# One image's group norm issued as three steps instead of one, its square on another engine, and a new order of issue

## The chip, the cores and the metric

The kernel runs on one core of a Trainium2 chip. A core has five engines that work side by side, each through its own instruction queue in order: TensorE (PE, with its weight loads PEld), VectorE (DVE), ScalarE (ACT), GpSimd (POOL), and SyncE (SP), which here only issues DMA transfers. Engines wait for each other through semaphores. The metric is the time of the whole launch on the device in microseconds (us); lower is better.

## The reference

The input is 16 images of 64 x 64 pixels with 128 channels, float32. Two layers follow each other, each a residual around a group norm over 32 groups of 4 channels:

```
g = v.reshape(B_, H_, W_, G, C_ // G)
m = mean(g, axis=(1, 2, 4));  s = var(g, axis=(1, 2, 4))
_gn(v) = (g - m) / sqrt(s + 1e-5)

x = x + L0(_gn(x))        # layer 0: a two-dimensional recurrent cell over rows and columns
x = x + L1(_gn(x))        # layer 1: a selective state space model (Mamba), forward and backward
```

Layer 1 flattens an image to 4096 tokens. Both directions share the weights. Per direction: a projection to 256 inner channels and a depthwise convolution of 4 taps with silu give `xc`; from `xc` come a small `dt` (softplus), and 16 values each of B and C per token. For each of 256 channels and 16 states a recurrence runs over the tokens,

```
h = exp(dt * A) * h + dt * B * xc
y = sum over states of h * C   (+ xc * D)
```

and `y` times a silu gate is projected back to 128 channels. The two directions are added.

## The kernel before

**Layer 0** takes the first 1,500 us or so: a wavefront over the diagonals of the images, eight images at a time. The square of its norm is the same code as in layer 1. Its cell has a product on GpSimd (L892) beside one on VectorE (L893).

**Layer 1** is the rest. An image is 16 passes: eight chunks of 512 tokens forward (the first half), then the same eight backward (the second half). A chunk is held as two halves of 128 channels on the partitions. For each pass and half, the exponentials `da` (L1248, "decay") are made by ScalarE; the recurrence of one state over 512 tokens is one VectorE scan (L1305, 32 a pass). Four of the 16 states (those below NX) get `dt*x*B` from GpSimd (L1256, `group`), the other twelve from TensorE by diagonal matrices (L1285, `hps`). Twelve products with C are made by GpSimd (L1328, `hc`), two states each; with `dt*x` (L1229) and four products with B that is 18 GpSimd instructions a pass. TensorE sums the states by transposing (L1365). The last value of each scan goes by a small DMA from SP (L1317, "keep") to `carry`, for the next pass. A pair of scans shares a buffer `hst`, of which there are three.

**The next image's norm.** While image b is scanned, image b+1 is read chunk by chunk (read_load, read_turn, read_take, read_stats): loaded, transposed by TensorE, copied to `xT` by ScalarE, and its statistics taken by VectorE (L1061). When all eight are there, `normal` (L1063) combines them and calls `group_norm` (L730): mean over the four channels of a group by a matmul, deviation on VectorE, its square on ScalarE, variance by two matmuls, square root on ScalarE (L743), reciprocal and shift on VectorE. Then `normalise` (L1073) applies scale and shift to the eight chunks on ScalarE. There are 15 such norms in the scan layer, one for each image but the first, whose norm ends layer 0. ScalarE's functions lie in tables; the square root's and the exponential's are not loaded together.

**The order of the work** is written by a planner that runs before the kernel is built. `order_of_issue` lists every operation of layer 1 with its engine, a cost from the table COST, what it comes after, and which ring buffers it takes and releases; `simulate` plays them and picks on each engine, whenever it is free, the ready operation with the lowest key. The key is NS times the pass number plus a number from the table URGENCY, one for each operation of a pass and for each half. An operation may have a `table`; then TABLE (1.28) is added where ScalarE's table changes. The result is one list in which all engines' instructions are issued; on the chip each engine works through its part in order, and a waiting instruction holds up all behind it. Three PSUM banks ("bank") are shared by transposes, projections and the decays of four states.

To the planner `normal` is one operation of VectorE of 3.0 us without a table, although it also issues TensorE's and ScalarE's parts at that place.

Of the kernel before, what the change touches and what calls it, by code (L numbers as in the profile page):

```python
# [9 lines left out]
AF = mybir.ActivationFunctionType  # L10
ALU = mybir.AluOpType
# [33 lines left out]
def units_of(order):  # L45

    count = {}
    for x in order:
# [4 lines left out]
        else:  # L53
# [18 lines left out]
    "read_take": 0.56, "read_stats": 0.69, "normal": 3.0, "normalise": 0.75, "spread": 0.6, "rows": 1.0,  # L72
# [18 lines left out]
        {(0, 0): 68.37, (0, 1): 99.65, (0, 2): 79.28, (0, 3): 203.77, (1, 0): -114.87, (1, 1): -118.67,  # L91
         (1, 2): -126.73, (1, 3): -118.24},
        {(0, 0): 155.27, (0, 1): 154.99, (0, 2): 240.19, (0, 3): 214.32, (1, 0): -240.9, (1, 1): -234.27,
         (1, 2): -200.93, (1, 3): 192.92},
    ),
    "xproj": (
        {(): -10.97},
        {(): 44.2},
    ),
    "xproj_take": (  # L100
        {(): -8.7},
        {(): 67.11},
    ),
    "rows": (
        {(): -153.13},
        {(): -118.25},
    ),
    "bturn": (
        {(): 62.15},
        {(): 213.27},  # L110
    ),
    "bturn_take": (
        {(): 172.77},
        {(): 178.75},
    ),
    "dtproj": (
        {(0,): -204.87, (1,): -204.87},
        {(0,): -241.05, (1,): -56.88},
    ),
    "times": (  # L120
        {(0,): -244.38, (1,): 220.24},
        {(0,): -131.05, (1,): -34.21},
    ),
    "turn": (
        {(0,): 249.35, (1,): 249.17},
        {(0,): -12.52, (1,): 136.36},
    ),
    "turn_take": (
        {(0,): 225.5, (1,): 225.64},
        {(0,): 168.68, (1,): 229.12},  # L130
    ),
    "scaled": (
        {(0,): 241.23, (1,): 249.64},
        {(0,): -126.09, (1,): 207.32},
    ),
    "skip": (
        {(0,): 219.33, (1,): 133.55},
        {(0,): -198.84, (1,): 234.94},
    ),
    "spread": (  # L140
        {("b", 0): 100.66, ("d", 0): 113.55, ("c", 0): -191.38, ("c", 1): -175.48, ("d", 1): -182.63,
         ("c", 2): -137.51, ("c", 3): 194.71, ("b", 1): 239.03, ("d", 2): -6.3, ("c", 4): 205.44, ("c",
         5): 205.67, ("k", 0): 249.62},
        {("b", 0): -196.06, ("d", 0): -21.03, ("c", 0): 95.8, ("c", 1): 217.74, ("d", 1): -173.2, ("c",
         2): -224.87, ("c", 3): -109.91, ("b", 1): 32.51, ("d", 2): 68.11, ("c", 4): 105.18, ("c", 5):
         250, ("k", 0): 106.72},
    ),
    "drive": (
        {(0, 0): -29.51, (1, 0): -31.7, (0, 1): 248.1, (1, 1): 247.61},
        {(0, 0): -30.69, (1, 0): -14.83, (0, 1): 76.36, (1, 1): 227.82},  # L150
    ),
    "decay": (
        {(0, 0): 118.09, (4, 0): 46.1, (5, 0): 43.31, (6, 0): 225.59, (7, 0): 236.9, (1, 0): 231.93, (8,
         0): 212.64, (9, 0): 250, (10, 0): 220.73, (11, 0): 230.04, (2, 0): 219.52, (12, 0): 250, (13,
         0): 243.2, (14, 0): 242.1, (15, 0): 236.57, (3, 0): 92.3, (4, 1): 244.91, (5, 1): 245.08, (6,
         1): 230.56, (7, 1): 235.88, (0, 1): 94.2, (8, 1): 250, (9, 1): 250, (10, 1): 249.86, (11, 1):
         249.41, (1, 1): 240.77, (12, 1): 94.69, (13, 1): 246.36, (14, 1): 95.9, (15, 1): 250, (2, 1):
         250, (3, 1): 250},
        {(0, 0): 143.92, (4, 0): 173.94, (5, 0): 235.37, (6, 0): 166.71, (7, 0): 249.54, (1, 0): 211.4,
         (8, 0): 218.32, (9, 0): 181.78, (10, 0): 227.93, (11, 0): 238.08, (2, 0): -85.83, (12, 0):  # L160
         229.6, (13, 0): 219.86, (14, 0): 178.16, (15, 0): 196.66, (3, 0): 76, (4, 1): 209.87, (5, 1):
         236.73, (6, 1): 35.09, (7, 1): 155.05, (0, 1): 65.39, (8, 1): 246.13, (9, 1): 249.07, (10, 1):
         45.55, (11, 1): 213.12, (1, 1): 199.94, (12, 1): 249.37, (13, 1): 240.07, (14, 1): 201.6, (15,
         1): 223.57, (2, 1): 139.92, (3, 1): 139.64},
    ),
    "scan": (
        {(0, 0): -143.97, (4, 0): -144.41, (5, 0): -203.2, (6, 0): -177.82, (7, 0): -185.62, (1, 0):
         -181.51, (8, 0): -237.82, (9, 0): -224.86, (10, 0): -250, (11, 0): -238.04, (2, 0): -238.15,
         (12, 0): -228.87, (13, 0): -229.22, (14, 0): -249.94, (15, 0): -248.9, (3, 0): 6.49, (4, 1):
         138.6, (5, 1): 138.89, (6, 1): 21.72, (7, 1): 20.73, (0, 1): 168.47, (8, 1): 100.86, (9, 1):  # L170
         72.61, (10, 1): 93.86, (11, 1): 202.9, (1, 1): -199.43, (12, 1): -147.92, (13, 1): -148.63, (14,
         1): -181.73, (15, 1): -152.26, (2, 1): -134.86, (3, 1): -124.94},
        {(0, 0): -214.33, (4, 0): -219.13, (5, 0): -218.95, (6, 0): -219.13, (7, 0): -140, (1, 0):
         -246.02, (8, 0): 208.31, (9, 0): 184.92, (10, 0): 207.89, (11, 0): 205.81, (2, 0): 205.48, (12,
         0): 229.6, (13, 0): 227.38, (14, 0): 227.3, (15, 0): 227.84, (3, 0): 210.13, (4, 1): 203.18, (5,
         1): 190.13, (6, 1): 196.98, (7, 1): 248.22, (0, 1): 44.78, (8, 1): 44.3, (9, 1): 53.53, (10, 1):
         53.41, (11, 1): 53.08, (1, 1): 229.32, (12, 1): 226.23, (13, 1): -82.64, (14, 1): -82.71, (15,
         1): -47.78, (2, 1): -33.84, (3, 1): -110.83},
    ),
    "scatter": (  # L180
        {("d", 0): -100.64, ("d", 1): 95.72, ("d", 2): -159.12, ("k", 0): 102.97},
        {("d", 0): -25.83, ("d", 1): 239.18, ("d", 2): -120.64, ("k", 0): 187.06},
    ),
    "drive_rows": (
        {(0, 0): -75.98, (1, 0): 210.15, (2, 0): 159.44, (0, 1): -216.43, (1, 1): 95.52, (2, 1): 115.92},
        {(0, 0): 175.76, (1, 0): 119, (2, 0): -243.29, (0, 1): -177.54, (1, 1): 61.32, (2, 1): 235.16},
    ),
    "keep": (
        {(0, 0): 232.07, (1, 0): 115.13, (2, 0): 84.57, (3, 0): -18.36, (4, 0): 78.14, (5, 0): -150.63,
         (0, 1): 129.78, (1, 1): 176.01, (2, 1): -242.19, (3, 1): -198.85, (4, 1): 171.84, (5, 1): 202.73},  # L190
        {(0, 0): -91.43, (1, 0): 202.39, (2, 0): 250, (3, 0): -79.2, (4, 0): -18.6, (5, 0): 222.86, (0,
         1): -21.3, (1, 1): 184.5, (2, 1): -137.27, (3, 1): -121.94, (4, 1): -128.43, (5, 1): 158.96},
    ),
    "out_of": (
        {(0, 0): 220.21, (1, 0): 220.3, (2, 0): 247.6, (3, 0): 247.25, (4, 0): -116.32, (5, 0): -229.45,
         (0, 1): -18.17, (1, 1): -15.17, (2, 1): -16.71, (3, 1): -16.75, (4, 1): -16.1, (5, 1): -15.52},
        {(0, 0): -8.58, (1, 0): -16.15, (2, 0): 69.62, (3, 0): 56.3, (4, 0): 227.32, (5, 0): 43.54, (0,
         1): -112.29, (1, 1): -195.82, (2, 1): -184.49, (3, 1): -212.68, (4, 1): -240.92, (5, 1): 67.09},
    ),
    "sums": (  # L200
        {(0, 0): -96.07, (1, 0): 249.75, (2, 0): 243.85, (3, 0): 61.49, (4, 0): 172.81, (5, 0): -65.92,
         (0, 1): 147.15, (1, 1): 40.49, (2, 1): 16.98, (3, 1): -10.84, (4, 1): -198.17, (5, 1): -49.98},
        {(0, 0): -224.96, (1, 0): -243, (2, 0): -210.02, (3, 0): -250, (4, 0): -246.13, (5, 0): -82.21,
         (0, 1): 103.84, (1, 1): 150.23, (2, 1): 247.44, (3, 1): 191.91, (4, 1): 200.85, (5, 1): 136.54},
    ),
    "keep_group": (
        {(0, 0): -22.23, (0, 1): -187.05},
        {(0, 0): -239.66, (0, 1): -160.74},
    ),
    "turned": (  # L210
        {(0, 0, 0): -144.95, (0, 0, 1): 152.62, (0, 0, 2): -158.13, (0, 0, 3): -41.49, (0, 1, 0):
         -190.27, (0, 1, 1): -150.04, (0, 1, 2): -93.55, (0, 1, 3): -142.02},
        {(0, 0, 0): -247.79, (0, 0, 1): 84.82, (0, 0, 2): 79.27, (0, 0, 3): -247.36, (0, 1, 0): 202.59,
         (0, 1, 1): 200.35, (0, 1, 2): 199.96, (0, 1, 3): 200.1},
    ),
    "turned_take": (
        {(0, 0, 0): 25.04, (0, 0, 1): 26.28, (0, 0, 2): 24.39, (0, 0, 3): 95.62, (0, 1, 0): 136.51, (0,
         1, 1): 250, (0, 1, 2): 248.1, (0, 1, 3): 250},
        {(0, 0, 0): 88.31, (0, 0, 1): 231.98, (0, 0, 2): 231.27, (0, 0, 3): 200.95, (0, 1, 0): 171.58,
         (0, 1, 1): 167.45, (0, 1, 2): 165.18, (0, 1, 3): 210.27},  # L220
    ),
    "weigh": (
        {(0, 0): -37.82, (0, 1): 224.4},
        {(0, 0): 108.42, (0, 1): 136.29},
    ),
    "finish": (
        {(0,): 151.14, (1,): 250},
        {(0,): 141.5, (1,): -236.48},
    ),
    "spill": (  # L230
        {(): -28.08},
        {},
    ),
    "read_load": (
        {(): -189.73},
        {},
    ),
    "read_turn": (
        {(): -56.24},
        {},  # L240
    ),
    "read_take": (
        {(): 23.65},
        {},
    ),
    "read_stats": (
        {(): 53.18},
# [53 lines left out]
def order_of_issue(images):  # L301
# [27 lines left out]
    get = done.get  # L329
# [1171 lines left out]
```

## Time and profile before

| what | value |
|---|---|
| median of 3 runs | 12480.04 us (12465.78 to 12492.38) |
| the profiled execution's own time | 12473.08 us |
| its span | 12471.1 us |
| mean granted TensorE clock | 0.985 |
| busy: PE, DVE, ACT, POOL | 11816.2, 11102.2, 10217.3, 10573.6 us |
| one image in the scan layer | about 682 us |

The span is the time from the first instruction to the last. Busy time is that of an engine's own instructions; an idle time is put down to what ended it ("<-"). In a timeline a row is the start in us, the duration, the engine, the line, the operation with its tiles, and how many instructions were merged; in brackets stands the idle time before it and its releaser. In a table of stretches each engine has its busy time and, in brackets, its number of instructions.

### The profile page before, as it was taken

Reading aid. Unit: us, or ns where it says so; the run is one execution under the profiler, and the core shown is the slowest. Engines: PE = TensorE matmul, PEld = TensorE weight load, DVE = VectorE, ACT = ScalarE, POOL = GpSimd, SP = SyncE. Lnnn points to the kernel's source line nnn. Section 1 sums busy time; section 2 is a strip of 40 time slices with the busy share of each in tenths; the row PEclk is TensorE's granted clock in tenths of the full one; section 3 lists DMA queues with packets and bytes.
Section 4 is the critical chain, followed back from the end, with each engine's and each line's share of the span. In section 5 each row is a group of like instructions: output and inputs, shape, how many; then the busy total and the mean of one; then the engine's idle time right before and its main releaser. Section 6 shows DMA issues by size and latency. Waiting matters only on the chain. (4 is left out here: it accounts for less than half of the span.)

```text
span 12471.1 us, 314271 instructions
## 1 busy us (share of the span) xinstructions
PE 11816.2 (95%) x123700; PEld 9141.1 (73%) x123700; DVE 11102.2 (89%) x11407; ACT 10217.3 (82%) x16448; POOL 10573.6 (85%) x4868
## 2 busy tenths in 40 slices
PE   9999989999999989899999999998999999999989
PEld 8656867777777767677777777776777777777777
DVE  7767589899999999999999999999999999999989
ACT  3444588888888888888888888888888888898888
POOL 0111199999999999999999999999999999999999
PEclk9999899999999999999999999999999999999999
DMA  4222255555555555555555555555555555555555
GB/s 156 56 56 56 56 152 167 159 166 161 163 167 157 169 158 164 158 170 158 165 163 163 160 164 167 155 167 158 167 158 169 160 162 164 163 165 162 163 154 149
DMA packets 2333045, 1885.43 MB, mean 151 GB/s; under 512 B 1549985, under 2 KB 1895601, under 8 KB 2331569
## 3 DMA queue, kind: packets, MB, share of 16 engines
q1 hardware_dynamic: 2253616, 1830.09, 51.0%
q10 hardware_dynamic: 77952, 35.24, 1.2%
q8 instruction: 977, 16.01, 0.5%
q14 instruction: 500, 4.09, 0.1%
HBM read 1698.25 MB, written 164.30 MB: 149 GB/s over the span
## 5 line engine op out<-in xcount | busy, mean ns | idle before, releaser
L1328 POOL TENSOR_TENSOR hc<-hst,cr 128x1024 f32<-128x1024 f32 x3072 | 7391.7, 2432 | 421.5 <-DVE hst L1305 303.8
L1305 DVE TENSOR_TENSOR_SCAN hst<-da,carry,hps 128x512 f32<-128x512 f32 x5376 | 6449.9, 1261 | 489.5 <-issue 188.4
L1248 ACT ACTIVATE da<-dt,A_log_sb 128x512 f32<-128x512 f32 x8192 | 5409.2, 711 | 805.3 <-DVE hst L1305 717.8
L1365 PE MATMUL py<-ident,hc 128*128 128x128 f32 x24576 | 3207.3, 277 | 31.8 <-POOL hc L1328 30.9
L1365 PEld LDWEIGHTS py<-ident,hc 128*128 128x128 f32 x24576 | 2812.4, 143 | 516.2 <-issue 346.6
L1256 POOL TENSOR_TENSOR group<-dtx,br 128x1024 f32<-128x1024 f32 x1024 | 2464.3, 2408 | 19.8 <-DMA br<-rows 10.4
L1305 DVE TENSOR_TENSOR_SCAN group<-da,carry,group 128x512 f32<-128x512 f32 x1792 | 2234.4, 1266 | 161.0 <-ACT da L1248 159.8
L1285 PEld LDWEIGHTS hps<-d,dtxt 32*128 32x128 f32 x49152 | 1545.4, 189 | 936.2 <-issue 583.1
L1285 PE MATMUL hps<-d,dtxt 32*128 32x128 f32 x49152 | 1835.7, 286 | 395.6 <-issue 237.0
L1127 PE MATMUL pp<-xT,wk 128*128 128x512 f32 x4096 | 1946.3, 595 | 0.9 <-DVE xl L913 0.5
L1345 ACT COPY ht<-ptg 128x512 f32<-128x512 f32 x2048 | 1125.7, 588 | 322.5 <-PE ptg L1337 290.3
L892 POOL TENSOR_TENSOR a_f<-a_f,c 128x16 f32<-128x16 f32 (+35 forms) x254 | 188.4, 742 | 1320.4 <-ACT a_f L884 1258.0
L1337 PE MATMUL ptg<-ident,group 128*128 128x128 f32 x8192 | 1193.6, 281 | 59.8 <-ACT ht L1345 33.8
L1337 PEld LDWEIGHTS ptg<-ident,group 128*128 128x128 f32 x8192 | 935.6, 143 | 283.4 <-issue 98.8
L1127 PEld LDWEIGHTS pp<-xT,wk 128*128 128x128 f32 x4096 | 696.9, 191 | 487.5 <-issue 481.0
L1305 DVE TENSOR_TENSOR_SCAN hst<-da,hps 128x512 f32<-128x512 f32 x768 | 875.3, 1200 | 77.1 <-issue 41.0
L1229 POOL TENSOR_TENSOR dtx<-dt,xc 128x512 f32<-128x512 f32 x512 | 651.7, 1288 | 124.8 <-ACT dt L1223 95.9
L1248 ACT ACT_TABLE_LOAD x527 | 676.1, 1283 | 9.3
L1352 PE MATMUL py<-ht,k 128*32 128x128 f32 x16384 | 568.0, 277 | 22.2 <-ACT ht L1345 22.2
L884 ACT ACTIVATE a_f<-pg_f,b_sb 128x16 f32<-128x16 f32 (+35 forms) x508 | 220.0, 473 | 419.1 <-DMA x<-xl 208.7
L1213 PE MATMUL pv<-dbl,dt_wT 128*128 128x256 f32 x2048 | 531.4, 392 | 0.0
L1352 PEld LDWEIGHTS py<-ht,k 128*32 128x32 f32 x16384 | 414.0, 110 | 112.0 <-issue 43.2
(113 smaller groups left out, 12180.2 us busy)
## 6 DMA issues: line engine op xcount, KB each, us to landing
cr<-rows SPq DMA_DIRECT2D x1536, 512.0 KB
d<-d SPq DMA_DIRECT2D x768, 448.0 KB
br<-rows SPq DMA_DIRECT2D x512, 512.0 KB
k<-k SPq DMA_DIRECT2D x256, 256.0 KB
yf<-y SPq DMA_DIRECT2D x128, 512.0 KB
yl<-yf SPq DMA_DIRECT2D x128, 512.0 KB
carry<-hst SPq DMA_DIRECT2D x3072, 1.0 KB
xs<-in_x_dram SPq DMA_DIRECT2D x64, 512.0 KB
```

Source lines behind the costliest of these rows:

```text
L1127: nc.tensor.matmul(self.ps["conv", h], lhsT=wk[:, k, h * P : (h + 1) * P], rhs=xT[self.b % 2][:, t0 : t0 + T], start=(k == 0), stop=(k == ...
L1213: nc.tensor.matmul(pv[:, q * TQ : (q + 1) * TQ], lhsT=dt_wT[:, q, h * P : (h + 1) * P], rhs=self.dbl, start=True, stop=True,)
L1229: nc.gpsimd.tensor_mul(self.dtx[h], self.dt[h], self.xc[h])
L1248: nc.scalar.activation(t, self.dt[h], AF.Exp, scale=amat[:, h, s : s + 1])
L1256: nc.gpsimd.tensor_mul(both[:, m : m + 2, :], bc(self.dtx[h], 1, 2), self.brow[q])
L1285: nc.tensor.matmul(part[:, j, :, :], lhsT=self.dtxt[h][rows, j, :], rhs=dg[rows, j + r, :, :], start=True, stop=True, skip_group_check=True,)
L1305: nc.vector.tensor_tensor_scan(t[:, self.rev], self.da.pop((s, h))[:, self.rev], dbx[:, self.rev], 0.0 if self.first else carry[:, self.d, ...
L1328: nc.gpsimd.tensor_mul(self.hc[g, h], self.hst[g, h].rearrange("p t m -> p m t"), self.crow[g])
L1337: nc.tensor.transpose(pt[:, k, :], self.group[g, h][:, t0 : t0 + TB, :].rearrange("p t s -> p (t s)"), ident,)
L1345: nc.scalar.copy(t, self.ps.pop(("turned", g, h, j)))
L1352: nc.tensor.matmul(self.py[h][q * TB : (q + 1) * TB, j * P : (j + 1) * P], lhsT=cd[:, GX * j + q, :], rhs=self.ht[g, h, j][:, q, :], start ...
L1365: nc.tensor.matmul(self.py[h][:, cols], **{"start": False, "stop": False, **how}, skip_group_check=True)
```

## The change

The function `group_norm` is cut into `variance` (up to the variance in PSUM), `root` (the square root) and `affine` (reciprocal and shift). In the scan layer the three are separate operations for the planner: `normal` of 1.9 on VectorE, `root` of 0.26 on ScalarE with the table "sqrt", `affine` of 0.32 on VectorE. The PSUM bank is held until `affine` has read it. Layer 0 and the first image still call all three in a row. The square is a product on VectorE instead of an activation on ScalarE. All numbers of URGENCY are new, so the order of the whole scan layer is planned anew. The product dt*x stays on GpSimd.

```diff
-    "read_take": 0.56, "read_stats": 0.69, "normal": 3.0, "normalise": 0.75, "spread": 0.6, "rows": 1.0,
+    "read_take": 0.56, "read_stats": 0.69, "normal": 1.9, "root": 0.26, "affine": 0.32, "normalise": 0.75, "spread": 0.6, "rows": 1.0,
...
 URGENCY = {
...
     "scatter": (
-        {("d", 0): -100.64, ("d", 1): 95.72, ("d", 2): -159.12, ("k", 0): 102.97},
-        {("d", 0): -25.83, ("d", 1): 239.18, ("d", 2): -120.64, ("k", 0): 187.06},
+        {("d", 0): -168.23, ("d", 1): 82.53, ("d", 2): -166.69, ("k", 0): 97.09},
+        {("d", 0): -57.95, ("d", 1): 171.82, ("d", 2): -166.2, ("k", 0): 182.23},
     ),
...
     "normal": (
         {},
-        {(): 52.85},
+        {(): -21.8},
+    ),
+    "root": (
+        {},
+        {(): -78.05},
+    ),
+    "affine": (
+        {},
+        {(): -45.32},
     ),
     "normalise": (
         {},
-        {(): 87.21},
+        {(): 117.4},
     ),
...
                     put("normal", (), "DVE", who=b + 1, key=("normal", b + 1),
                         after=[get((f, b + 1, k)) for k in range(NCH) for f in ("read_take", "read_stats")], takes=[m],
-                        uses=[m])
+                        uses=[])
+                    tiles[m][1] += 1
+                    put("root", (), "ACT", who=b + 1, key=("root", b + 1), after=[get(("normal", b + 1))])
+                    ops[-1]["table"] = "sqrt"
+                    put("affine", (), "DVE", who=b + 1, key=("affine", b + 1), after=[get(("root", b + 1))])
+                    ops[-1]["uses"].append(m)
                 put("normalise", (n - NCH,), "ACT", who=b + 1,
-                    after=[get(("normal", b + 1))])
+                    after=[get(("affine", b + 1))])
...
-    def group_norm(pool, mv, n, tag, bank):
-
+    def variance(pool, mv, n, tag, bank):
...
-        nc.scalar.activation(sq, dev, AF.Square)
+        nc.vector.tensor_mul(sq, dev, dev)
         nc.tensor.matmul(pv, lhsT=gavg, rhs=sq, start=True, stop=False)
         nc.tensor.matmul(pv, lhsT=gavg, rhs=mv[:, :, 1], start=False, stop=True)
+        return pm
+
+    def root(pool, pm, n, tag):
+
         std = pool.tile([P, n], F32, name=f"std_{tag}", tag="gn_std")
-        nc.scalar.activation(std, pv, AF.Sqrt, bias=eps)
+        nc.scalar.activation(std, pm[:, 1, :], AF.Sqrt, bias=eps)
+        return std
+
+    def affine(pool, pm, std, n, tag):
+
         scale = pool.tile([P, n], F32, name=f"scale_{tag}", tag="gn_scale")
         nc.vector.reciprocal(scale, std)
         shift = pool.tile([P, n], F32, name=f"shift_{tag}", tag="gn_shift")
-        nc.vector.scalar_tensor_tensor(shift, mean, -1.0, scale, ALU.mult, ALU.mult)
+        nc.vector.scalar_tensor_tensor(shift, pm[:, 0, :], -1.0, scale, ALU.mult, ALU.mult)
         return scale, shift
...
         def normal(b, place=None):
             mv = gp.tile([P, 1, 2], F32, name=f"mv_{b}", tag="mv")
             nc.vector.bn_aggr(mv[:, 0, :], norm[b].rearrange("p n s -> p (n s)"))
-            norm[b] = group_norm(
-                gp, mv, 1, f"l1_{b}", lambda name, shape: bank(place, name, shape)
-            )
+            norm[b] = variance_of(gp, mv, 1, f"l1_{b}", lambda name, shape: bank(place, name, shape))
+
+        def root(b):
+            norm[b] = norm[b], root_of(gp, norm[b], 1, f"l1_{b}")
+
+        def affine(b):
+            norm[b] = affine_of(gp, *norm[b], 1, f"l1_{b}")
```

## The prediction

> **What bounds the kernel now.** I read the groups of instructions first. In the scan layer GpSimd does the two products of each state pair, and their rows are the largest:
>
> ```profile
> L1328 POOL TENSOR_TENSOR hc<-hst,cr 128x1024 f32<-128x1024 f32 x3072 | 7391.7, 2432 | 421.5 <-DVE hst L1305 303.8
> ...
> L1256 POOL TENSOR_TENSOR group<-dtx,br 128x1024 f32<-128x1024 f32 x1024 | 2464.3, 2408 | 19.8 <-DMA br<-rows 10.4
> ```
>
> With the 651.7 us of dt*x (L1229) that is 10,508 us. GpSimd's first product of this layer starts at 1,539 us and the last ends at 12,461, so it is busy 96% of 10,922 us. A pass has 18 such instructions, about 41 us. What is left to win is its idle time. So I cut image 10 (8,368 to 9,051 us) into stages; the columns are length, then busy time (count) of PE, PEld, DVE, ACT and POOL, then TensorE clock and DMA:
>
> ```profile
> 8452.10:8502.00 49.90, 42.60 (x489) 34.29 (x489) 42.92 (x40) 46.67 (x73) 42.22 (x20) 0.93 0.53 151
> ...
> 8543.70:8711.00 167.30, 147.97 (x1728) 114.49 (x1726) 150.31 (x126) 141.09 (x221) 158.96 (x72) 0.98 0.56 154
> 8711.00:9051.50 340.50, 337.86 (x3760) 264.75 (x3757) 318.56 (x281) 296.59 (x461) 326.69 (x145) 0.99 0.58 168
> ```
>
> The last line is the eight passes of the second half: PE is busy 337.9 of 340.5 us, POOL 326.7. They run at PE's pace and have nothing to give. The middle line is four passes of the first half, close to POOL's pace. The first line is the pass in which the next image's norm lies: 49.9 us instead of about 41.5, and no engine is full. What a first half costs without the next image's reads and norm is seen in the last image, which has none (first line below) against the image before it:
>
> ```profile
> 11777.60:12115.30 337.70, 307.53 (x3531) 240.39 (x3530) 305.54 (x259) 290.44 (x457) 324.20 (x146) 0.97 0.56 154
> 11095.50:11439.50 344.00, 310.28 (x3570) 241.91 (x3569) 311.41 (x271) 303.37 (x477) 324.00 (x145) 0.98 0.56 157
> ```
>
> So reads, norm and normalising together cost 6.3 us an image, 15 times: 95 us is the most that a better border can bring with the rest as it is. Then the timeline of one border (image 14), by engine, VectorE first, ScalarE next, GpSimd last:
>
> ```profile
> 11180.48 0.35 DVE L1065 BATCH_NORM_AGGREGATE mv<-st 128x2 f32<-128x48 f32 x1
> 11182.63 0.16 DVE L737 TENSOR_TENSOR dev_l<-mv,pm_l 128x1 f32<-128x1 f32 x1 [1.80 <-PE pm_l L735]
> 11184.63 0.16 DVE L745 RECIPROCAL scale_l<-std_l 128x1 f32<-128x1 f32 x1 [1.84 <-ACT std_l L743]
> 11184.83 0.16 DVE L747 SCALAR_TENSOR_TENSOR shift_l<-pm_l,scale_l 128x1 f32<-128x1 f32 x1
> 11184.91 4.79 DVE L1305 TENSOR_TENSOR_SCAN hst<-da,carry,hps 128x512 f32<-128x512 f32 x4
> 11189.99 2.46 DVE L1305 TENSOR_TENSOR_SCAN group<-da,carry,group 128x512 f32<-128x512 f32 x2 [0.29 <-ACT da L1248]
> 11193.15 1.28 DVE L1305 TENSOR_TENSOR_SCAN group<-da,carry,group 128x512 f32<-128x512 f32 x1 [0.70 <-ACT da L1248]
> ```
> ```profile
> 11182.82 0.20 ACT L739 ACTIVATE sq_l<-dev_l 128x1 f32<-128x1 f32 x1 [1.79 <-DVE dev_l L737]
> 11183.04 1.28 ACT L743 ACT_TABLE_LOAD   x1
> 11184.34 0.26 ACT L743 ACTIVATE std_l<-pm_l,eps 128x1 f32<-128x1 f32 x1
> ```
> ```profile
> 11187.53 4.79 POOL L1328 TENSOR_TENSOR hc<-hst,cr 128x1024 f32<-128x1024 f32 x2 [3.35 <-DVE hst L1305]
> 11197.01 2.43 POOL L1328 TENSOR_TENSOR hc<-hst,cr 128x1024 f32<-128x1024 f32 x1 [4.69 <-DVE hst L1305]
> ```
>
> VectorE is held from 11,180.48 to 11,184.99, 4.51 us without a scan: 1.80 idle for TensorE's mean, 1.84 for ScalarE's root. ScalarE idles 1.79 for the deviation. GpSimd then starves twice, 3.35 and 4.69 us; the other borders show the same pair.
>
> **The change part by part**, for one border, then times 15.
>
> *The hold of VectorE.* It loses the 1.84 us wait for the root, with the two last operations, which come later as a step of their own (0.36 us), and gains the square (0.16 us, the row of the deviation, same shape). The wait of 1.80 for the mean stays: the matmul stands in TensorE's queue behind its 32 block products. Counted so, VectorE gains 1.84 - 0.16 = 1.68 us.
>
> [...] The square multiplies the deviation by itself, both in SBUF; the deviation before it and the scans have an input in PSUM. [...]
>
> ```profile
> 993.48 1.19 POOL L892 TENSOR_TENSOR a_f<-a_f,c 128x472 f32<-128x472 f32 x1 [6.88 <-ACT a_f L884]
> ...
> 993.98 1.19 DVE L893 TENSOR_TENSOR a_f<-a_f,c 128x472 f32<-128x472 f32 x1 [1.84 <-ACT a_f L884]
> 995.27 0.65 DVE L895 TENSOR_TENSOR a_f<-a_f,a_f 128x472 f32<-128x472 f32 x1
> ```
>
> The same shape costs VectorE 1.19 us beside GpSimd and 0.65 alone; it ends 0.5 us after GpSimd's. In the scan layer GpSimd's instructions last 2.43 us, one after another. At the end of the 15 deviations the running one had between 0.12 and 1.94 us to go, mean 1.29. [...] I take 1.45: the hold becomes 4.51 - 1.84 - 0.36 + 1.45 = 3.76, the two last operations are paid later, and VectorE gains 0.4 us, not 1.7. Affine may also wait: nothing if the root is done when its turn comes, up to 1.84 if it is planned too early; I take 0.2 for it. Left: 0.2 us.
>
> *ScalarE.* The square and the idle time ahead of it go: 0.20 + 1.79 = 1.99 us. The root comes as a step of its own. The planner thinks that the variance is there 1.9 + 0.2 us after the norm starts; by the rows above it is there after 2.3 (deviation) + 1.45 + 0.4 (two matmuls) = 4.2. If the root is issued as soon as the plan allows, ScalarE waits the difference of 2.1 less the table load of 1.28 ahead of it, 0.8. Behind it stand the normalising steps and the decays that VectorE's scans wait for. So it gains 1.2 (bounds: 0 to 2.0). What that is worth: after the border VectorE waits 0.29 + 0.70 = 1.0 us for decays, so at most 1.0.
>
> *Table loads.* There is one for the root and one back to the exponential, 1.28 us each, as now; the plan before charged neither, the plan after charges both. A root set beside a table switch of the silu or softplus steps saves one. [...] I take the trace and a chance of one half: 0.65.
>
> *Hidden edits.* None of the three steps issues a DMA. The norms of the first layer (two) and the first image's also square on VectorE; a few tenths once each, in a span of 12,471: nothing. The PSUM bank is held from the mean to affine, some 6 us instead of 3; two of the three banks stay for the others. Bounds 0 to 1 us an image, taken as 0: if the cover of TensorE's backlog is gone, it is GpSimd that waits.
>
> *The order.* All urgencies are new, so every queue may differ: SP's keeps, scatters and spreads among them. I can't derive the order by reading. The second half is held by PE's sum of work whatever the order, the first by GpSimd's. I cost it at nothing, from -3 us an image (half of the 6.3) to +6 (second rival).
>
> **Sum.** 0.2 + 1.0 + 0.65 = 1.85 us x 15 = 28 us. The profiled execution took 12,473.1 us, its span 12,471.1 with 2 us around it; 12,473 - 28 = 12,445. The median of the runs shown is 7 us above that execution, so about 12,450.
>
> **The rivals.**
> *The border closes.* If the plan with its true costs also places decays and normalising so that GpSimd keeps its backlog, both gaps go: the bound is 95 us, 12,385. For it: ScalarE is busy 46.7 of 49.9 us there. Against: VectorE still does eight statistics of 0.67 us and the norm, about 9 us more than a plain pass, with 3 us of slack a pass.
> *The new order makes SP late, and it ends slower.* VectorE's rows of waits hold 157 us in all for `carry<-hst`: the small transfers that keep a last state, issued by SP in order, behind scatters that take 2.8 us for four. A scan pair can't write its buffer (three of them) until that transfer has read it. In the last image three first-half passes take 44.2 to 44.7 us for this, against 41.5. Two more passes of this kind in each of 16 images cost 2 x 2.7 x 16 = 86, less the 28: 12,540. It decides from about one such pass an image (2.7 against 1.85 us).
> [...]
>
> **How the numbers follow.** Within 0.2% (25 us) a measurement of this kernel can hardly tell a change from none. Forecast 0.35, its own range 12,420 to 12,470, of which four fifths lie below 12,455; border closed 0.14; stall only moved 0.16; SP late 0.35. Faster: 0.28 + 0.14 = 0.42. Same: 0.07 + 0.16 = 0.23. Slower: 0.35. The range goes from just below the border's bound, 12,380, to 12,580, which leaves the worst of the SP case, three and more passes, outside.
>
> **What would show it.** The hold from the aggregate to the square's end near 3.8 us, with the square's row well above 0.16 us (mean 1.0 to 1.5). No idle of 1.8 us ahead of the reciprocal. The root's row with a wait below 1 us; 527 + 256 + 255 + 18 table loads or some 8 fewer. The pass with the norm at 47 to 48 us, the second half at 340. I am wrong if VectorE's waits for `carry<-hst` rise well above 157 us, if second-half passes leave 42.5 us, or if the square stays at 0.16 and the pass falls below 45.

## The result, and the profile after

The changed kernel takes 12,517.9 us (median of six, 12,505.8 to 12,527.7), the kernel before on the same chip 12,471.0 (12,461.0 to 12,492.4): a ratio of **1.0035 (95% interval 1.0025 to 1.0045)**. It is slower by some 45 us, where 28 us faster were forecast. The time lies inside the range given, on the wrong side.

The profiled execution of the changed kernel, its fastest, has a span of 12,504.1 us against 12,471.1. The difference of 33 us is the sum of three: the scan layer begins at 1,551.1 instead of 1,539.0 us (+12, see the last section), the sixteen first halves take 5,479.1 instead of 5,497.5 (-18), the second halves 5,463.5 instead of 5,424.3 up to the last GpSimd product (+39; the tail behind it is 10.4 us in both). A pass is 18 GpSimd products, from the start of its first to that of the next pass's first. Images and passes are counted from 0: pass 2 is the third, pass 8 the first of the second half. Mean lengths over images 1 to 14, in us:

| profile | pass 1 | pass 2 (norm) | passes 3 to 7 together | pass 8 |
|---|---|---|---|---|
| before | 43.5 | 49.8 | 210.0 | 41.9 |
| changed | 45.9 | 50.0 | 206.4 | 43.8 |

So the pass with the norm, in which the whole gain was to appear, has not become shorter. The stretches of image 10 in the changed kernel, with the same columns as for the kernel before (length, busy time and count of PE, PEld, DVE, ACT, POOL, then TensorE clock, DMA share and GB/s): pass 2, and the second half.

```profile
8468.80:8518.60 49.80, 42.48 (x486) 32.57 (x487) 44.33 (x40) 44.59 (x70) 41.73 (x20) 0.97 0.54 147
...
8726.90:9068.60 341.70, 336.85 (x3737) 262.70 (x3737) 316.70 (x279) 294.75 (x458) 325.24 (x146) 1.00 0.57 167
```

ScalarE lost 2.1 us of busy time in that pass (46.67 before), but the pass still takes 49.8 us. The timeline of the border in image 14 shows what took its place. VectorE:

```profile
11209.89 0.34 DVE L1092 BATCH_NORM_AGGREGATE mv<-st 128x2 f32<-128x48 f32 x1
11210.76 0.15 DVE L751 TENSOR_TENSOR dev_l<-mv,pm_l 128x1 f32<-128x1 f32 x1 [0.54 <-PE pm_l L749]
11210.95 1.83 DVE L753 TENSOR_TENSOR sq_l<-dev_l 128x1 f32<-128x1 f32 x1
...
11216.24 0.13 DVE L767 RECIPROCAL scale_l<-std_l 128x1 f32<-128x1 f32 x1
...
11219.86 4.80 DVE L1336 TENSOR_TENSOR_SCAN hst<-da,carry,hps 128x512 f32<-128x512 f32 x4 [3.29 <-PE hps L1316]
```

The waits for the mean (1.80 us) and the root (1.84) have shrunk to 0.54 and to none. The square takes 1.83 us, and it ends at 11,212.78. GpSimd's timeline tells why: the second of its two products there ends at 11,212.77.

```profile
11208.04 4.73 POOL L1287 TENSOR_TENSOR group<-dtx,br 128x1024 f32<-128x1024 f32 x2 [0.15 <-PE ptx L1267]
```

At all 15 borders of this profile the square ends within 0.02 us of the GpSimd instruction that was running when it started. From the aggregate's start to the square's end it is 2.9 us here and 2.7 in the mean, instead of 4.5 for the old hold, in which the two last operations took 0.36. But 7 us later there is a new wait of 3.29 us for block products. TensorE's timeline at the same border tells where it comes from:

```profile
11210.37 0.35 PE L749 MATMUL pm_l<-mv,gavg 128*128 128x1 f32 x2 [0.16 <-DVE mv L1092]
11212.83 0.38 PE L754 MATMUL pm_l<-sq_l,gavg 128*128 128x1 f32 x2 [2.11 <-DVE sq_l L753]
...
11214.88 3.75 PE L1158 MATMUL pp<-xT,wk 128*128 128x512 f32 x6
11218.56 1.17 PE L1316 MATMUL hps<-d,dtxt 32*128 32x128 f32 x32
```

The variance matmul stands at the head of TensorE's queue and waits 2.11 us for the square. Behind it stand the six convolution matmuls and the block products of the next scans. And the six matmuls take 3.75 us; at the seven borders of images 1 to 14 where the clock stays full they take 2.74. The table of stretches around them has the reason in its third column from the right, the granted clock:

```profile
11210.00:11213.00 3.00, 0.73 (x6) 0.47 (x4) 2.43 (x4) 2.98 (x4) 3.00 (x3) 1.00 0.64 55
11213.30:11218.60 5.30, 5.30 (x20) 3.01 (x19) 3.23 (x5) 4.88 (x7) 4.25 (x2) 0.68 0.88 290
```

TensorE was busy 0.73 of 3.0 us, and in the 5.3 us after that it has a mean clock of 0.68 (1.00 is the full clock). GpSimd, which starved for 3.35 and 4.69 us at this border before, now starves for 4.73 and 5.60:

```profile
11222.46 4.80 POOL L1359 TENSOR_TENSOR hc<-hst,cr 128x1024 f32<-128x1024 f32 x2 [4.73 <-DVE hst L1336]
11232.85 2.41 POOL L1287 TENSOR_TENSOR group<-dtx,br 128x1024 f32<-128x1024 f32 x1 [5.60 <-PE ptg L1368]
```

Over the whole kernel TensorE's waits for the square, in total, times and longest, are 29.1 us; before (for ScalarE's square) they were 7.8:

```profile
PE pm_l L754 <- DVE sq_l L753: 29.1, 15, 2.4
```

### The profile page after: what moved, and what is told of

Same layout as the page of the kernel before. It is cut to its first block, busy times and chain, and to the rows that moved or that the text cites. A ratio compares the mean times of both kernels' runs of the same rounds, so it can differ in the third digit from the quotient of the medians.

```text
span 12504.1 us, 314081 instructions
## 1 busy us (share of the span) xinstructions
PE 11840.6 (95%) x123700; PEld 9126.2 (73%) x123700; DVE 11116.3 (89%) x11425; ACT 10215.8 (82%) x16430; POOL 10577.5 (85%) x4868
## 3 DMA queue, kind: packets, MB, share of 16 engines
q1 hardware_dynamic: 2253616, 1830.09, 50.9%
```

## The experiments

The theory after the result, **QUEUE**: the square is late because VectorE waits for GpSimd, and the price is paid through TensorE's in-order queue, not through VectorE's own hold. Against it: that the *order* is at fault (the "SP late" rival, or pass 8), that *VectorE's hold* is what counts, or that ScalarE's work behind the norm does. The texts written ahead of the runs name these theories: NORM is QUEUE under its first name, before VectorE's hold was told apart from it; ORDER, HOLD and ACT are the three against it; SPLIT blames the PSUM bank that is held longer and the root's new place; CLOCK comes with the question of TensorE's clock. In the end one question was left: why 1.4 us more of waiting lengthen the pass by about 2.5 us. The runs went to several chips, on which the kernel before took 12,474 to 12,581 us, so only ratios to the kernel before on the same chip are compared, with their 95% intervals.

**The new order alone** (root and affine issued directly behind the variance, the square on ScalarE as before):

```diff
+        yield op
+        if op[0] == "normal":
+            yield "root", op[1], (), []
+            yield "affine", op[1], (), []
...
-        nc.vector.tensor_mul(sq, dev, dev)
+        nc.scalar.activation(sq, dev, AF.Square)
```

> The new order with the norm as it was before: root and affine issued directly behind the normal step, the square on ScalarE. Theory ORDER (the loss lies in the new order: the pass before the norm +2.4 us, the first pass of the second half +1.9 us an image): as slow as the changed kernel or slower, 12,510 to 12,550 us. Theory NORM (the loss comes from the square that waits for GpSimd and holds TensorE's queue for 1.9 us): about the kernel before, 12,460 to 12,480 us.

Measured: 1.0000 (0.9991 to 1.0008), pass 2 at 48.2 us. The order is not what makes the kernel slower.

**The old order on the new kernel** (the URGENCY of the kernel before for all old steps, the new values for root and affine):

> The three steps and the square on VectorE, planned with the urgencies of before (root and affine with those of the changed kernel). Theory ORDER: the second half is back at 338.5 us, the norm costs what it did or less, 12,440 to 12,475 us. Theory NORM: the square waits here too, 1.3 us and TensorE behind it, 12,490 to 12,520 us.

Measured: 1.0113 (1.0098 to 1.0128). This run did not isolate the norm. With two operations added, the planner moves hundreds of instructions (554 of TensorE's 12,408 operations have to be moved to get from one order to the other), and passes 2, 3 and 7 grew to 52.7, 46.1 and 44.8 us; in passes 3 and 7 of image 8 GpSimd waits 4.6 and 5.1 us for transposes of `group`. It suggests that a set of urgencies fits one list of operations only. For later runs the finished order was edited.

**The square in other forms, all else as changed.** First back on ScalarE:

```diff
-        nc.vector.tensor_mul(sq, dev, dev)
+        nc.scalar.activation(sq, dev, AF.Square)
```

> The changed kernel with the three steps and the new order, only the square back on ScalarE. [...] Rival SPLIT (holding the PSUM bank longer and the new place of the root are the loss, since the new order with a whole norm stood at 1.000): stays at 1.003 to 1.005.

Then on VectorE, but with the second operand as a scalar per partition, which at one column is the same arithmetic:

```diff
-        nc.vector.tensor_mul(sq, dev, dev)
+        (nc.vector.tensor_scalar_mul if n == 1 else nc.vector.tensor_mul)(sq, dev, dev)
```

> The changed kernel, but in the scan layer the square is the deviation times itself as a per-partition scalar, so that the instruction has one SBUF tensor instead of two. Theory NORM: the square's row falls from 1.6 us to below 0.2, TensorE's wait for it from 1.9 us to 0.3, VectorE's wait for the next block products (1.6 us) goes too; 1.5 to 3 us an image, 12,470 to 12,495 us. Theory ORDER: the same row, but within 12 us of the changed kernel, since GpSimd's gaps come from elsewhere. [...]

> The changed kernel with the scalar form of the square, again, beside the three others on one chip. All theories: ratio 0.9986 as before, within 0.001.

And the changed kernel once more beside the run on ScalarE:

> The changed kernel itself, on the same chip as the three runs beside it. Both theories: ratio to the kernel before 1.0035, as measured first; a chip whose carry transfers land later may shift it by 0.001.

Measured: ScalarE 0.9993 (0.9984 to 1.0002); scalar form 0.9986 (0.9978 to 0.9995), and again 0.9983 (0.9974 to 0.9992); changed again 1.0026 (1.0014 to 1.0038). The intervals of the changed form and of both others lie apart. **The form of one instruction of 0.2 us, 15 times, costs 0.4 to 0.5% between the two forms on VectorE**, and 0.33% against the square on ScalarE on the same chip; the scalar form beats both kernels. The tile view of the square, in the changed kernel and then with the scalar form (ns min/median/max):

```profile
L753 DVE TENSOR_TENSOR sq_l<-dev_l x18: 146/1636/2110, 63.8 to 11211.0; 128x1 f32<-128x1 f32 x16, 128x8 f32<-128x8 f32 x2
```
```profile
L753 DVE TENSOR_SCALAR sq_l<-dev_l x16: 205/214/214, 1455.0 to 11244.2; 128x1 f32<-128x1 f32 x16
```

In the scalar form 14 of the 15 squares of the scan layer's borders started with 1.6 us or more of a GpSimd instruction still to run, and each took 0.21 us. With the square on ScalarE, in image 8 (aggregate at 7,145.00), TensorE waits 0.48 us and the block products start 5.4 us after the aggregate; in the border of image 14 shown above it was 8.7:

```profile
7146.34 0.38 PE L754 MATMUL pm_l<-sq_l,gavg 128*128 128x1 f32 x2 [0.48 <-ACT sq_l L753]
...
7150.38 1.17 PE L1316 MATMUL hps<-d,dtxt 32*128 32x128 f32 x32
```

**Is it the queue or VectorE's hold?** The two variance matmuls are issued later, behind the next block products; the root follows them, affine and normalising come two scans later. Once with the two-tensor square, once with the scalar form:

```diff
-        nc.tensor.matmul(pv, lhsT=gavg, rhs=sq, start=True, stop=False)
-        nc.tensor.matmul(pv, lhsT=gavg, rhs=mv[:, :, 1], start=False, stop=True)
-        return pm
+        def products():
...
+        if image is not None and name == "drive_rows":
+            yield "products", image, (), []
+            yield "root", image, (), []
```

> The changed kernel, its square still a product of two SBUF tensors; only the two matmuls that take the square stand behind the next block products in TensorE's queue, the root behind them, and the last part two scans later. Theory QUEUE (the loss is TensorE standing 1.9 us for the square, which makes the next block products late for VectorE): the square's row stays at 1.6 us, TensorE has no wait for it, VectorE's wait of 1.6 us for block products behind the norm is gone, and the pass with the norm falls from 50 or 51 us to 48.5: ratio 0.998 to 1.000. Theory HOLD (the loss is VectorE standing still 1.5 us longer): stays at 1.002 to 1.0035.

> As the run before it, with the scalar form of the square. Theory QUEUE: the same time as the tensor form within 0.0005, since nothing waits for the square any more: 0.998 to 1.000. Theory HOLD: 0.998, and 0.003 below the tensor form.

Measured: 0.9997 (0.9988 to 1.0007) and 0.9996 (0.9987 to 1.0006), pass 2 at 48.5 and 47.8 us. The two-tensor square still takes 1.73 us in the mean and still holds VectorE, yet the loss is gone: a square for which TensorE's queue doesn't stand still cost nothing that could be measured here. The theory QUEUE holds against HOLD. (That they are 0.1% slower than the scalar form without this move may be due to ScalarE, which now waits for the late variance, 2.0 to 2.3 us in the scalar one of the two and 2.0 to 3.8 in the other; this was not tried by itself.)

This run also sorts the +39 us of the second halves. Here, on a chip where the kernel before takes 12,478 us, they still take 5,463 us, while the first halves take 5,464 (5,498 in the kernel before, 5,479 in the changed kernel, both on the first chip). As far as two chips can be compared, the new order takes time from the first halves and puts about as much into the second; the square's loss lies in the first.

**The other half: TensorE's clock.** By the profiles, the borders of the changed kernel fall into two kinds: in some the clock is halved for 3.4 us or more within 9 us of the aggregate (0.50 from 11,213.50 to 11,216.91 in image 14), in some it isn't. With the square on ScalarE, in the scalar form, or with the late matmuls, it never was. Means over images 1 to 14:

| profile | square, us | borders with halved clock | block products after the aggregate, us | pass 2, us |
|---|---|---|---|---|
| changed | 1.65 | 7 of 14 | 7.7 | 50.0 |
| changed again | 1.64 | 9 of 14 | 8.2 | 51.0 |
| changed, third | 1.73 | 10 of 14 | 8.3 | 50.8 |
| square on ScalarE | 0.20 | none | 5.4 | 48.3 |
| scalar form | 0.21 | none | 5.4 | 48.4 |

Within the changed kernel's three profiles, borders at full clock have their block products after 6.5 to 6.7 us and passes of 49.0 to 49.3; those with the halved clock 8.6 to 9.2 us and 50.9 to 51.9.

Which border was hit went with where its wait fell. In these profiles the granted clock changes only at the marks of a fixed grid of 3.41 us. Images 4 and 7 of the first profile each wait 1.92 us for the square. In image 4 most of it falls into one stretch of the grid (4,369.78 to 4,373.19): TensorE is busy there for 1.33 us, and the next stretch has half the clock. In image 7 TensorE is busy for 1.96 us of the stretch from 6,424.61 to 6,428.02, and the clock stays full. At the 26 halved borders of the table TensorE was busy for 23 to 53% of the stretch just before the fall; at the 16 others its least busy stretch around the wait has 55 to 87%. So the number of borders that were hit is in part chance: 7, 9 and 10 of 14 in three executions of one kernel.

To see whether the clock is a cause or a companion, TensorE got products of the identity, which nothing reads, to fill its idle spell. Seven of them ahead of the deviation, with both forms of the square:

```diff
+        for _ in range(7 if warm else 0):
+            nc.tensor.matmul(room[:, P:], lhsT=ident, rhs=ident, start=True, stop=True)
         dev = pool.tile([P, n], F32, name=f"dev_{tag}", tag="gn_dev")
```

> The changed kernel beside the two runs that follow, for the same chip. Its profile should again show two kinds of border: those where TensorE's clock stays full in the 9 us after the aggregate (first block products 6.5 to 6.7 us after it, the pass with the norm 49.2 to 49.3 us) and those where it is halved for 3.4 us or more (8.6 to 9.2 us, pass 50.9 to 51.9). About half of each. Ratio to before 1.0026 to 1.0035.

> The changed kernel with seven 128x128 products of the identity put into TensorE's queue between the mean's matmul and the square's; nothing reads their result. They fill some 1.6 of the 1.9 us for which TensorE stands idle, so the matmul of the square still comes at the same time, only the idle spell is gone. Theory CLOCK (the idle spell makes the chip halve TensorE's clock just behind it, and that is more than half of the loss): no border has a halved clock in the 9 us after the aggregate, the first block products come 6.5 to 6.9 us after it in every image, the pass with the norm takes 49.2 to 49.5 us, and the kernel is 0.10 to 0.20% faster than the changed one beside it (ratio to before about 1.001). Rival QUEUE ALONE (the late matmul costs the whole loss, the halved clock is a companion that costs nothing): the pass stays at 50 to 51 us and the ratio that of the changed kernel.

> The same seven products in the kernel with the square in its scalar form (0.21 us, no wait for GpSimd). Now the products themselves hold the square's matmul back, by some 1.0 to 1.4 us, at full clock, while VectorE isn't held. If what counts is when TensorE's queue goes on, and its clock, this is as warm_tensor: block products about 6.5 us after the aggregate, pass 49 us, ratio about 1.000 to 1.001. If VectorE's own hold of 1.4 us counts, it is 0.1% or more below warm_tensor, at the 0.9985 of the scalar form without the products.

Measured: changed 1.0026 (1.0015 to 1.0037); two-tensor form 1.0042 (1.0029 to 1.0056); scalar form 1.0007 (0.9998 to 1.0016). The two-tensor form missed its aim: the deviation waited for the products, as VectorE's timeline of image 14 shows, and the square then met GpSimd's next instruction.

```profile
11311.92 0.15 DVE L755 TENSOR_TENSOR dev_l<-mv,pm_l 128x1 f32<-128x1 f32 x1 [2.21 <-PE pm_l L753]
11312.11 2.32 DVE L757 TENSOR_TENSOR sq_l<-dev_l 128x1 f32<-128x1 f32 x1
```

TensorE still idled 2.60 us there. The scalar form was near what was expected of its passes: block products 7.1 us after the aggregate, no halved clock, pass 2 at 49.4. But its deviation waited for the products too, so that VectorE was held for 3.0 us from the aggregate to the square's end; as a test of VectorE's hold this run doesn't count. Then six products behind the deviation, which leave the deviation and the square where they were:

```diff
         nc.vector.tensor_sub(dev, mv[:, :, 0], mean)
+        for _ in range(6 if warm else 0):
+            nc.tensor.matmul(room[:, P:], lhsT=ident, rhs=ident, start=True, stop=True)
```

> In the run with seven products of the identity the deviation waited for them (2.21 us instead of 0.54), so the square came 1.7 us later and met the next instruction of GpSimd. Here six such products (some 1.55 us) are issued behind the deviation: it stays where it was, the square too, and TensorE's idle spell of 1.9 us ahead of the square's matmul shrinks to two short ones below 0.6 us. Theory CLOCK: no border with a halved clock in the 9 us after the aggregate; first block products 6.5 to 7.1 us after it in every image, the pass with the norm 49.0 to 49.5 us where the changed kernel has 50.8 to 51.0, and a ratio to before of 1.0005 to 1.0015. Rival QUEUE ALONE: the pass stays at 50.5 to 51 us, the ratio at 1.0025 or above, with or without a halved clock.

Measured: 1.0007 (0.9998 to 1.0016). TensorE's timeline in image 14, where the aggregate starts at 11,211.58:

```profile
11212.68 1.61 PE L755 MATMUL pm_l<-ident 128*128 128x128 f32 x12 [0.25 <-DVE dev_l L753]
11214.37 0.38 PE L758 MATMUL pm_l<-sq_l,gavg 128*128 128x1 f32 x2
...
11215.74 2.74 PE L1162 MATMUL pp<-xT,wk 128*128 128x512 f32 x6
11218.41 1.17 PE L1320 MATMUL hps<-d,dtxt 32*128 32x128 f32 x32
```

The square takes 1.65 us here (1.43 in the mean) and the variance matmul comes 2.8 us after the aggregate, as in the mean of the changed kernel; but the convolution takes 2.74 us instead of 3.75. In all 14 images the clock stays full, the block products come 6.8 us after the aggregate in the mean, and pass 2 takes 49.1 us. **Work that nobody needs made the pass shorter here, since it kept TensorE's clock**: 49.1 us is what the changed kernel's own borders at full clock take. For the whole kernel the evidence is thinner, for the changed kernel did not run on that chip: the interval lies below that of the changed kernel on the first chip (1.0025 to 1.0045) and overlaps those on the other two by 0.0002 (from 1.0014). So by the ratios the loss has two halves: from the scalar form (0.9985) to the late matmul at full clock (1.0007) 0.22%, from there to the changed kernel (1.0026 to 1.0035) 0.19 to 0.28%, each uncertain by about 0.1%.

**A GpSimd product of pass 8**, which had grown by 1.9 us: its third product with B, which waits there, is issued later:

```diff
+        if name == "drive" and args == (0, 1) and who % NP == NCH:
+            held = op
+            continue
```

> The changed kernel with one GpSimd instruction moved: in the first pass of each second half the third product with B is issued behind two products with C, where the kernel before has it; it waits there for a group buffer today (1.7 to 3.3 us). Theory ORDER, if this instruction is the cause in that pass: that pass falls from 43.8 us to about 42, 1.9 us x 15 = 28 us, 12,490 us. If the pass is held by TensorE's queue: the gap only moves and the time stays at 12,510 to 12,525 us.

Measured: 1.0057 (1.0041 to 1.0074). A miss: pass 8 grew to 47.6 us. In image 8 GpSimd's wait there went from 3.7 us for a transfer of `carry` (changed again) to 5.1 us for VectorE, which waits 6.6 us for TensorE's block products. The longer pass 8 belongs to the new order, which pays for it elsewhere: with the new order alone it is 44.7 us, and that kernel is as fast as before.

**The split in the old order.** The finished order of the kernel before, root right behind the variance, affine and normalising two scans later, with either form of the square:

```diff
+        if name == "normal":
+            yield op
+            yield "root", who, (), []
...
+            if scans == 2:
+                yield "affine", image, (), []
+                yield from held
```

> The order of before, instruction by instruction; only the root stands directly behind the norm's first part and the last part two scans later, ahead of the normalising steps, and the square is made on VectorE from one SBUF tensor and a per-partition scalar. Theory NORM: VectorE is held 2.6 us instead of 4.3 and GpSimd's two gaps shrink by 1.7 us or more, 15 x 1.7 = 26 us: ratio 0.997 to 0.999. Rival SPLIT: 1.001 to 1.004.

> As the run before it, but the square is a product of two SBUF tensors as in the changed kernel. Theory NORM: the square's row is 1.3 us on average (0.2 to 2.1), TensorE stands still for it, and the gain is lost: 1.2 us x 15 = 18 us or more above the run with the scalar form, ratio 0.999 to 1.002. If both runs agree within 0.0005, the square's wait costs nothing in this order.

Measured: 1.0010 (1.0003 to 1.0017) and 1.0016 (1.0008 to 1.0024). The hold became shorter, and nothing was won, as the rival SPLIT had said for the first of them (1.001 to 1.004). The square's form hardly counts in this order: the two runs are 0.06% apart, within their intervals, though the two-tensor square takes 0.73 us in the mean. With the scalar form, VectorE stops 5 us later for the decays, and GpSimd's second gap is 7.1 us:

```profile
6468.14 2.46 DVE L1343 TENSOR_TENSOR_SCAN group<-da,carry,group 128x512 f32<-128x512 f32 x2 [2.63 <-ACT da L1286]
```
```profile
6475.15 2.42 POOL L1366 TENSOR_TENSOR hc<-hst,cr 128x1024 f32<-128x1024 f32 x1 [7.07 <-DVE hst L1343]
```

**Normalising spread out** (one step behind every second decay), in the kernel before, in the split old order and in the scalar form of the new one:

```diff
+        if op[0] == "normalise":
+            held.append(op)
+            continue
...
+            if decays % 2 == 0:
+                yield held.pop(0)
```

> The kernel before, with one thing changed: the eight normalising steps of the next image are issued one behind every second decay, instead of four in a row right behind the norm. Theory ACT (at the border ScalarE's late decays set when VectorE and then GpSimd go on): the second gap of GpSimd shrinks from 4.7 us to 2 or 3, 15 x 2 to 3 = 30 to 45 us, ratio 0.996 to 0.998. Rival HOLD (VectorE's 4.3 us without a scan alone set both gaps): 0.9995 to 1.0005.

> The order of before with the norm in three parts and the scalar form of the square, and the normalising steps one behind every second decay. Theory ACT: VectorE's wait of 2.6 us for decays behind the last part goes, GpSimd's second gap falls from 7.1 us to 3 or 4; against the same kernel with the normalising in a row (ratio 1.001) 3 to 4 us x 15 = 45 to 60 us, ratio 0.996 to 0.998. Rival HOLD: no change, 1.001.

> The new order with the three parts and the scalar form of the square, and the normalising steps one behind every second decay. Theory ACT: there VectorE has no wait for decays behind the norm, only the pass after has; 0 to 1 us an image, ratio 0.998 to 0.9985. If the new order suffers from the same row of normalising steps as the old: 0.996.

Measured: 1.0037 (1.0025 to 1.0048), 1.0006 (0.9996 to 1.0015), 0.9997 (0.9987 to 1.0007). In the kernel before, the second gap shrank from 4.7 to 3.5 us, less far than expected, and new ones of 1.6 and 4.0 us came later, where the aggregate is at 6,475.32:

```profile
6490.64 2.42 POOL L1344 TENSOR_TENSOR hc<-hst,cr 128x1024 f32<-128x1024 f32 x1 [3.49 <-DVE hst L1321]
...
6510.57 4.79 POOL L1344 TENSOR_TENSOR hc<-hst,cr 128x1024 f32<-128x1024 f32 x2 [3.98 <-PE py L1381]
```

None of the three gains. A stall at the border that is taken from one engine turns up at the next. That the sum of ScalarE's work in that pass sets it is suggested by its 46.7 of 49.9 us, and wasn't shown.

## Why the prediction was wrong, point by point

- **The square's 1.45 us: right in size, counted in the wrong queue. This is the step that failed.** No run shows the 1.45 itself: it was the author's estimate, the 0.16 us of the row and the 1.29 us that GpSimd's running instruction had left in the mean. In the three profiles of the changed kernel the square takes 1.64 to 1.73 us in the mean, and at all 15 borders of the first profile it ends within 0.02 us of that GpSimd instruction. The prediction weighed this against VectorE's hold alone, found 0.2 us left, and stopped there. It never asked who takes the square next. That is TensorE, which idles 1.9 us for it with the convolution and the block products behind, and whose clock is then halved at half or more of the borders. The step should have read: block products 1.1 to 1.3 us later where the clock stays full and 2.3 to 2.9 us later in the mean of all borders, a pass of 50.0 to 51.0 instead of 48.3 us. At 2.7 us (changed again against the square on ScalarE, pass 2) times 15 that is 40 us; the two ratios differ by 0.33%, which is 41.
- **"The wait of 1.80 for the mean stays": wrong**, and to the good. In the new order it is 0.54 us. The hold is 2.7 us rather than the 3.76 predicted. The split runs in the old order and the late matmuls show that a shorter hold alone gains nothing.
- **ScalarE**: the square and its idle time are gone and the root waits 0.0 to 0.8 us, as said. That this is worth 1.0 us at VectorE was not borne out; the new wait for block products lies over it.
- **Table loads**: 527 + 256 + 255 + 18, unchanged. The 0.65 us were not won.
- **The order at nothing**: right as a sum (1.0000), by luck, through terms that cancel: in the changed kernel passes 1 and 8 grew by 2.4 and 1.9 us, passes 3 to 7 shrank by 3.6. The reason given for the second half, that TensorE's sum of work holds it whatever the order, is wrong: it grew from 339.0 to 341.5 us an image, while TensorE's busy time in image 10 fell from 337.86 to 336.85.
- **"SP late"** was given the same chance as the forecast and is wrong. On the first chip VectorE's waits for `carry<-hst` fell from 169.5 to 134.1 us (waits of the whole kernel, of which the prediction's 157 is a part). What came is of the kind that the chances call "stall only moved" (0.16): the square's 1.65 us went on to TensorE as a wait of 1.9 us. But there it was counted as the same time, and the kernel is 0.35% slower.
- **The size of the sum**: with the two halves of the loss taken away, the scalar form gives 0.14 to 0.17% (18 to 21 us) against the 28 forecast. That this is near the sum is luck as well: two of its three terms, ScalarE and the table loads, were not borne out.

## What to carry to other kernels

Price a wait not only on the engine that waits: follow its result into the queue of the engine that takes it, and count everything behind that instruction. If that engine is TensorE, ask also whether the idle spell costs it its clock; two idle microseconds were enough at 26 of 42 borders here. And an elementwise operation of one column with two SBUF tensors beside a busy GpSimd cost the rest of GpSimd's running instruction here (1.65 us in the mean, against 0.15 alone); a scalar operand did the same work in 0.21 us, without the wait. Change the order of issue and the operation in separate runs: the order, which looked the most dangerous, was innocent.

## What the runs showed of the hardware that was not expected

- **The scalar form did not wait for GpSimd.** `tensor_scalar` with its input and its scalar per partition both in SBUF took 205 to 214 ns in 16 of 16, the product of two tensors 0.15 to 2.4 us, depending on what GpSimd had left.
- **TensorE's clock fell after half-idle stretches.** In the changed kernel a spell with 0.73 us busy of 3.0 was followed by a halved clock (0.54 in the 3.4 us from 11,213.2). No stretch of the grid was wholly idle there: TensorE was busy for 1.14 of the 3.41 us up to the fall at 11,213.50, with 0.16 us idle ahead of the mean's matmul and 2.11 ahead of the square's. In the scan layer of the changed kernel's three profiles (from 1,600 us on) the clock fell 193 times, after stretches of the grid with TensorE busy for at most 55%; after the 9,176 others at full clock it stayed, and they have at least 41%. By the ratios above the halved clock cost 0.19 to 0.28% of the whole time, and together with the wait (0.22%) it decided the sign of the change.
- **The start of the kernel varies by execution.** The scan layer began at 1,550 to 1,556 us in five of the twenty profiles and at 1,532 to 1,542 in the others. In those five the granted clock between 60 and 120 us was 0.53 to 0.55, in the fifteen others 0.74 to 0.94. So the 12 us by which the scan layer began later in the changed kernel's profile are not the change's: the changed kernel began at 1,538.9 and 1,541.5 in its other two.
